# Attention energies from split queries and keys in one float32r pass, with keys and values streamed from DRAM

## The chip, the cores and the metric

The kernel runs on one core of one Trainium2 chip. A core has five engines that run their own instruction streams and meet at semaphores: TensorE (matrix products, PE in the profile; its weight loads are PEld), VectorE (DVE), ScalarE (ACT), GpSimd (POOL) and SyncE (SP), which here only issues DMAs. The metric is the device time of one execution in microseconds, the median of several runs.

## The reference, cut to what matters

Two layers on an image batch x of 4 x 64 x 64 pixels with 256 channels, all in float32. The first is full self-attention inside each image, with queries and keys of 32 channels:

```python
q = x @ Wq + bq            # 4 x 4096 x 32
k = x @ Wk + bk            # 4 x 4096 x 32
v = x @ Wv + bv            # 4 x 4096 x 256
energy = jnp.einsum('bnd,bmd->bnm', q, k)
attn = jax.nn.softmax(energy, axis=-1)
out = gamma * jnp.einsum('bnm,bmc->bnc', attn, v) + inputs
```

The second layer is a depthwise 3x3 convolution to 768 channels, two pointwise products with a GELU between them and a residual, and a local attention over each pixel's 3x3 window. The change touches the first layer only.

## The kernel before, in words

**Tiles and slots.** Each image has 4096 pixels in 8 blocks of 512 (NB). A slot is one block of queries; there are 32, in order, 8 for each image. In a slot the queries of the block meet the keys of all 8 blocks G of their image. The energies stand transposed: 128 keys on the partitions, 512 queries along the free axis. A group is one G: four matmuls (`energy`, L298 to 308) fill four PSUM banks `e` of 128 x 512; `weight` (L310) takes the exponential of two banks at a time on ScalarE into `p`; `product` (L315) multiplies each of the four key tiles' values with `p`, 128 x 512 at a time, into two accumulators `acc`; `add_up` (L329) sums `p` on VectorE into `den` for the softmax's denominator.

**The energies.** The contraction is only 32 long. The four tiles of keys of a block therefore sit in four strips of 32 partitions of one tile `ka` of 128 x 128, the queries are repeated in the four strips of `qa`, and each of the four matmuls uses its own strip of TensorE's rows (32*128 in the profile). They are float32 matmuls. The profile shows every float32 matmul of this kernel as two records.

**Where keys, queries and values come from.** `project_qk(s)` (L231) projects two blocks at once into one PSUM bank, `st` (L242) gets them with the bias added, and small DMAs on SP take the four strips of `ka` from `st` straight into SBUF (L254), 16 KB each, and the queries to a DRAM scratch `packed` (L259). `spread_queries` (L283) brings a block's queries from the scratch four times, into the four strips of `qa`, in the middle of the slot before. `project_v` (L263) makes the values of a block in two halves. Keys and values of a whole image stay in SBUF: 8 buffers of `ka`, 8 of `v`.

**Order of the work.** It is written out by hand. A slot has 16 points, two for each G. At the first of them `energy` is issued for the *next* group, so that the exponentials are a group ahead of the products; then come `weight`, a list of jobs of the second layer for slots further back (`jobs`), `product`, `add_up`, and on VectorE a number of steps of the convolution (`share`). Slots 7, 15 and 23 also project the next image (`nxt`): `project_v` of one block at every second point, `project_qk` of two blocks after the points 1, 5, 9 and 13, with their `xc` loads (L225) ahead. In slot 0 the same is squeezed in for the first image (`early_jobs`, `early`): blocks 0 and 1, then 2 and 3 ahead of the first energies, blocks 4 and 5 after point 1, blocks 6 and 7 after point 3.

**Queues.** Nearly all DMAs are issued on SP, in the order of the program: a DMA that has to wait for its source or for its buffer holds up all those behind it. A buffer of a rotating tile is free again when its last reader is done. On SP stand `renew` (L126, the next slot's block of x, at the start of a slot), the `xc` loads, the key and query copies above, and `out` stores of the second layer after points 4 and 5.

Of the kernel before, what the change touches and what calls it, by code (L numbers as in the profile page):

```python
# [8 lines left out]

F32 = mybir.dt.float32  # L10
AF = mybir.ActivationFunctionType
ALU = mybir.AluOpType
AX = mybir.AxisListType
# [24 lines left out]
GRP = P // CQK  # L38
NG = NT // GRP
SQ = 32  # L40
NJ = NB // SQ
NSLOT = B * NBLK
# [10 lines left out]
def attention_then_perception_kernel(  # L53
# [19 lines left out]
    nc = tc.nc  # L73
# [17 lines left out]
    def unshifted():  # L91
# [105 lines left out]


        queries, keys, values, staged = {}, {}, {}, {}
        packed = tc.dram_tile([CQK, B * N], F32, name="packed")  # L200

        def fetch(s):

# [27 lines left out]
        def project_qk(s):  # L231

            ps = bank("m", f"qk_{s}")
            for kin in range(CH):
                for r in range(2):
                    nc.tensor.matmul(  # L236
                        ps[2 * r * CQK : 2 * (r + 1) * CQK, :],
                        lhsT=wqk[:, kin].rearrange("p s d -> p (s d)"),
                        rhs=staged[s + r][:, kin, :], start=(kin == 0), stop=(kin == CH - 1),
                    )  # L240
            st = tile_of([P, NB], "st", f"st_{s}")
            nc.scalar.activation(st, ps, AF.Identity, bias=bqk2)  # L242
            if s == 0:
                queries[0] = tile_of([P, NB], "qa", "qa_0", 2)
                for j in range(GRP):
                    nc.sync.dma_start(
                        out=queries[0][j * CQK : (j + 1) * CQK, :], in_=st[:CQK, :]
                    )
            for r in range(2):
                at = 2 * r * CQK  # L250
                keys[s + r] = tile_of([P, P], "ka", f"ka_{s + r}", NBLK)
                queue = nc.sync if s + r else nc.scalar
                for j in range(GRP):
                    queue.dma_start(  # L254
                        out=keys[s + r][j * CQK : (j + 1) * CQK, :],
                        in_=st[at + CQK : at + 2 * CQK, bass.ts(j, P)],
                    )
                if s + r:
                    nc.sync.dma_start(  # L259
                        out=packed[:, bass.ts(s + r, NB)], in_=st[at : at + CQK, :]  # L260
                    )

        def project_v(s, pair, tag="m"):  # L263
            xc = staged[s]
            if pair == 0:
                values[s] = tile_of([P, TPB, C], "v", f"v_{s}", NBLK)
            ps = bank(tag, f"v_{s}_{pair}")
            for i in range(2):
                for kin in range(CH):
                    nc.tensor.matmul(  # L270
                        ps[:, i * C : (i + 1) * C],
                        lhsT=xc[:, kin, bass.ts(2 * pair + i, P)], rhs=wv[:, kin, :],
                        start=(kin == 0), stop=(kin == CH - 1),
                    )
            nc.scalar.copy(
                values[s][:, 2 * pair : 2 * pair + 2, :], ps.rearrange("p (t c) -> p t c", c=C)
            )

        def projections(s):
# [3 lines left out]
        def spread_queries(s):  # L283

            queries[s] = tile_of([P, NB], "qa", f"qa_{s}", 2)
            for j in range(GRP):
                nc.sync.dma_start(
                    out=queries[s][j * CQK : (j + 1) * CQK, :],
                    in_=packed[:, bass.ts(s, NB)],
                )  # L290


        energies, weights, sums, accs, lsums, lrdens = {}, {}, {}, {}, {}, {}
# [4 lines left out]
        def energy(s, G):  # L298

            e = epsum.tile([P, GRP, NB], F32, tag="e", name=f"e_{s}_{G}", bufs=1)  # L300
            key = keys[s - s % NBLK + G]
            for j in range(GRP):
                rows = slice(j * CQK, (j + 1) * CQK)
                nc.tensor.matmul(  # L304
                    e[:, j, :], lhsT=key[rows, :], rhs=queries[s][rows, :],
                    start=True, stop=True,
                )
            energies[s, G] = e

# [5 lines left out]
        def product(s, G, half):  # L315
            p = weights[s, G, half]
            first = G == 0 and half == 0
            if first:
                accs[s] = [bank("acc", f"acc_{s}_{c}") for c in range(CH)]
            v = values[s - s % NBLK + G]  # L320
            for i in range(2):
                for c in range(CH):
                    nc.tensor.matmul(  # L323
                        accs[s][c], lhsT=v[:, 2 * half + i, bass.ts(c, P)], rhs=p[:, i, :],
                        start=(first and i == 0),
                        stop=(G == NG - 1 and half == 1 and i == 1),
                    )
# [95 lines left out]
        percs, mixes, hids, hs = {}, {}, {}, {}  # L423
# [14 lines left out]
                thirds[:] = [t[:, i * NB : (i + 1) * NB] for i in range(3)]  # L438
            return thirds.pop(0)

        def spare(name):
            return tile_of([P, TPB, C], "v", name, NBLK).rearrange(
                "p (a t) c -> p a (t c)", a=2
            )

        def perceive(s, steps):

            at = ring(s) - 1
            percs.setdefault(s, {})

            def begin(i):
                if s >= NSLOT - LAG_PERC:

                    if i % 2 == 0:
                        percs[s, i] = spare(f"perc_{s}_{i}")
                    percs[s][i] = percs[s, i - i % 2][:, i % 2, :]
                else:
                    upper, j = divmod(i, MULT)
                    if not upper:
                        mixes[s, j] = perc_tile(f"perc_{s}_{j}")  # L460
                    percs[s][i] = mixes[s, j][:, 2 * upper : 2 * upper + 2, :].rearrange(
                        "p s n -> p (s n)"
                    )
                tap_of(i, 0, 0, RB)

            def tap_of(i, tap, r0, r1):
                half, j = divmod(i, MULT)
                dy, dx = divmod(tap, 3)
                acc = percs[s][i].rearrange("p (h w) -> p h w", w=W)[:, r0:r1, :]
                win = xv[:, half, at + dy + r0 : at + dy + r1, dx : dx + W]  # L470
                wt = wperc[:, half, j, tap : tap + 1]
                if tap == 0:
                    nc.scalar.activation(  # L473
                        acc, win, AF.Identity, bias=bperc[:, half, j : j + 1], scale=wt
                    )
                else:
                    nc.vector.scalar_tensor_tensor(acc, win, wt, acc, ALU.mult, ALU.add)  # L477

            for i, tap, *rows in steps:
# [227 lines left out]
        guides, lvs, near_ws, late, results, totals = [], {}, {}, {}, {}, {}  # L707
# [360 lines left out]
        for i in range(2):  # L1068
            project_v(1, i)
        project_qk(2)  # L1070
        energy(0, 0)
        weight(0, 0, 0)
        weight(0, 0, 1)
# [18 lines left out]
        for slot in range(NSLOT):  # L1092
# [3 lines left out]
            k, a = slot - LAG_HID, slot - LAG_ATT  # L1096
# [50 lines left out]
            for point in range(points):  # L1147
                G, half = divmod(point, 2)
                after = slot + (G + 1) // NG, (G + 1) % NG
                if half == 0:  # L1150
                    if G == NG // 2 and slot + 1 < NSLOT:
                        spread_queries(slot + 1)
                    if after[0] < NSLOT:
                        energy(*after)
# [515 lines left out]
```

## Time and profile before

| | |
|---|---|
| time, median of 3 runs | 3450.98 us (3450.44 to 3451.02) |
| span of the profiled execution | 3448.6 us |
| TensorE busy | 3437.1 us, 100% |
| VectorE busy | 2737.3 us, 79% |
| ScalarE busy | 1063.9 us, 31% |
| DMA, mean | 19 GB/s, 67.05 MB |
| products `acc` (L323) on TensorE | 1835.0 us, 4096 records |
| energies `e` (L304) on TensorE | 292.0 us, 2048 records |
| one plain slot (slots 5, 6, 8 and on) | 102.0 us |
| slots 7, 15, 23, which project the next image | 137.1 us |

The profiled execution's own time is its span; the unprofiled runs lie 2.4 us above it. In the profile a row such as `L304 PE MATMUL e<-qa,ka 32*128 32x512 f32` names the line of the kernel, the engine, the operation, the output and inputs by the program's names and the shape: 32 rows by 128 columns of the array, 512 columns moved. Matmuls are pipelined and their ends are modelled, so the distance between starts says how long TensorE was taken.

### The profile page before, as it was taken

How to read it: one execution, taken by the hardware profiler on the slowest of the kernel's cores; microseconds unless marked ns; L12 is line 12 of the kernel's file. 1: busy time of each engine (PE TensorE's matmuls, PEld its weight loads, DVE VectorE, ACT ScalarE, POOL GpSimd, SP SyncE). 2: the span in 40 equal slices, each digit the busy share in tenths (PEclk: the TensorE clock that was granted, in tenths of full speed). 3: DMA queues.
4: the chain of work that ended last, by engine and by line, in shares of the span. 5: the costliest groups of instructions: out<-in, count | busy, mean ns of one | idle time of the engine just before them, and what ended most of it. 6: DMA issues, size and time to landing. Idle time of an engine off the chain costs nothing.

```text
span 3448.6 us, 33677 instructions
## 1 busy us (share of the span) xinstructions
PE 3437.1 (100%) x12702; PEld 1991.7 (58%) x12702; DVE 2737.3 (79%) x4439; ACT 1063.9 (31%) x1328; POOL 365.7 (11%) x541
## 2 busy tenths in 40 slices
PE   9999999999999999999999999999999999999999
PEld 5445555556555556555555555566656555555555
DVE  2388888767888888876888888887688888888895
ACT  3232333323332233332333322333233333233331
POOL 2000001110111110111001111101110111110021
PEclk9999999999999999999999999999999999999999
DMA  4000000120000000012000000001100000000000
GB/s 107 7 4 10 7 10 16 28 47 18 16 13 10 16 16 16 21 26 46 16 10 16 10 13 16 16 22 29 43 16 16 16 10 7 16 16 18 7 7 26
DMA packets 93274, 67.05 MB, mean 19 GB/s; under 512 B 65872, under 2 KB 71248, under 8 KB 92976
## 3 DMA queue, kind: packets, MB, share of 16 engines
q1 hardware_dynamic: 92432, 64.42, 7.0%
q8 instruction: 102, 1.67, 0.2%
q14 instruction: 68, 0.56, 0.1%
q10 hardware_dynamic: 672, 0.39, 0.0%
HBM read 43.62 MB, written 18.81 MB: 18 GB/s over the span
## 4 chain that ended last, share of the span: by engine, by line
PE 98%; DVE 1%; DMA 0%; SPq 0%; ACT 0%; issue 0%; ACTq 0%; POOL 0%; DVEq 0%
PE acc L323 51%; PE e L304 8%; PE hid_de L582 5%; PE hid_gf L582 5%; PE hid_bc L582 5%; PE lv L895 3%; PE v L270 3%; PE lo L1029 3%; PE s L936 3%; PE hid_a L582 3%; PE dx_ab L534 2%; PE dx_cd L534 1%; PE dx_eg L534 1%; PE qk L236 1%; DVE perc L477 1%; PE dx_f L534 1%
## 5 line engine op out<-in xcount | busy, mean ns | idle before, releaser
L323 PE MATMUL acc<-p,v 128*128 128x512 f32 x4096 | 1835.0, 594 | 0.3 <-DVE o L388 0.3
L323 PEld LDWEIGHTS acc<-p,v 128*128 128x128 f32 x4096 | 768.1, 190 | 809.9 <-issue 793.0
L477 DVE SCALAR_TENSOR_TENSOR perc<-xp,wperc,perc 128x512 f32<-128x512 f32 (+2 forms) x1554 | 1104.5, 773 | 27.5 <-ACT perc L473 27.3
L312 ACT ACTIVATE p<-e 128x1024 f32<-128x1024 f32 x512 | 524.0, 1024 | 1714.9 <-PE e L304 710.7
L337 DVE TENSOR_TENSOR den<-den,p 128x1024 f32<-128x1024 f32 x480 | 587.2, 1223 | 86.2 <-ACT p L312 84.5
L961 POOL TENSOR_TENSOR lp<-lp,near 128x396 f32<-128x396 f32 x60 | 97.0, 1616 | 2487.8 <-ACT lp L956 2487.8
L304 PE MATMUL e<-qa,ka 32*128 32x512 f32 x2048 | 292.0, 640 | 0.0
L304 PEld LDWEIGHTS e<-qa,ka 32*128 32x128 f32 x2048 | 80.0, 182 | 166.2 <-issue 145.3
L582 PE MATMUL hid_de<-perc,wmix 128*128 128x256 f32 x720 | 165.2, 379 | 0.0
L582 PEld LDWEIGHTS hid_de<-perc,wmix 128*128 128x128 f32 x720 | 136.8, 190 | 43.7 <-issue 21.5
L483 DVE TENSOR_TENSOR perc<-perc 128x256 f32<-128x256 f32 x360 | 153.6, 441 | 8.2
L605 ACT ACTIVATE hid<-hid,bup 128x512 f32<-128x512 f32 x120 | 80.1, 714 | 219.5 <-DVE hid L589 219.5
L473 ACT ACTIVATE perc<-xp,bperc,wperc 128x512 f32<-128x512 f32 x192 | 145.3, 805 | 1.8 <-DVE xp L394 1.8
L984 POOL TENSOR_TENSOR lsum<-lsum,lp 128x99 f32<-128x99 f32 (+1 forms) x179 | 130.4, 735 | 11.7
L1029 PEld LDWEIGHTS lo<-lp,lv 128*128 128x128 f32 x732 | 102.9, 191 | 35.1 <-issue 27.2
L895 PE MATMUL lv<-wlv,h 128*128 128x256 f32 x520 | 122.4, 379 | 0.0
L589 DVE TENSOR_TENSOR hid<-hid_bc,hid 128x512 f32<-128x512 f32 x60 | 41.5, 692 | 101.7 <-PE hid_bc L582 101.7
L270 PE MATMUL v<-wv,xc 128*128 128x256 f32 x512 | 116.3, 380 | 0.3 <-DMA wv<-in_w_v 0.3
L270 PEld LDWEIGHTS v<-wv,xc 128*128 128x128 f32 x512 | 96.9, 190 | 28.4 <-issue 15.2
L936 PEld LDWEIGHTS s<-lq,h 128*128 128x128 f32 x520 | 87.1, 188 | 37.3 <-issue 27.4
L895 PEld LDWEIGHTS lv<-wlv,h 128*128 128x128 f32 x520 | 98.7, 190 | 15.5 <-issue 2.2
L1029 PE MATMUL lo<-lp,lv 128*128 128x99 f32 (+1 forms) x732 | 107.4, 295 | 0.0
(195 smaller groups left out, 3098.0 us busy)
## 6 DMA issues: line engine op xcount, KB each, us to landing
xp<-in_x SPq DMA_DIRECT2D x30, 528.0 KB, 4.1
xc<-in_x SPq DMA_DIRECT2D x56, 256.0 KB, 3.7
out<-lo SPq DMA_DIRECT2D x56, 256.0 KB, 2.0
qa<-packed SPq DMA_DIRECT2D x124, 64.0 KB, 2.1
out<-res SPq DMA_DIRECT2D x8, 256.0 KB, 2.0
ka<-st SPq DMA_DIRECT2D x124, 16.0 KB, 1.8
packed<-st SPq DMA_DIRECT2D x31, 64.0 KB, 1.9
wup<-in_w_up SPq DMA_DIRECT2D x1, 1536.0 KB, 6.9
```

What stands on the lines that cost most here:

```text
L270: nc.tensor.matmul(ps[:, i * C : (i + 1) * C], lhsT=xc[:, kin, bass.ts(2 * pair + i, P)], rhs=wv[:, kin, :], start=(kin == 0), stop=(kin = ...
L304: nc.tensor.matmul(e[:, j, :], lhsT=key[rows, :], rhs=queries[s][rows, :], start=True, stop=True,)
L312: nc.scalar.activation(p, energies[s, G][:, 2 * half : 2 * half + 2, :], AF.Exp)
L323: nc.tensor.matmul(accs[s][c], lhsT=v[:, 2 * half + i, bass.ts(c, P)], rhs=p[:, i, :], start=(first and i == 0), stop=(G == NG - 1 and hal ...
L337: nc.vector.tensor_tensor(den, den, p, ALU.add)
L477: nc.vector.scalar_tensor_tensor(acc, win, wt, acc, ALU.mult, ALU.add)
L483: nc.vector.tensor_tensor(t[:, to, :], t[:, a, :], t[:, b, :], op)
L534: nc.tensor.matmul(ps[:, n * C : (n + 1) * C], lhsT=w(j), rhs=values(j), start=(j == 0), stop=(j == kin - 1),)
L582: nc.tensor.matmul(ps[:, n * C : (n + 1) * C], lhsT=w(j), rhs=mixes[s, j][:, kind, :], start=(j == 0), stop=(j == MULT - 1),)
L895: nc.tensor.matmul(ps[:, half * C : (half + 1) * C], lhsT=keys_of(s, t, half, kin), rhs=wlv[:, kin, :], start=(kin == 0), stop=(kin == CH ...
L936: nc.tensor.matmul(ps[:, t * QR * QW : t * QR * QW + rows * QW].rearrange("p (h w) -> p h w", w=QW), lhsT=keys_of(s, t, half, kin), rhs=gu ...
L1029: nc.tensor.matmul(pv[:, rows, columns(half)], lhsT=lvs[block, t, half][:, bass.ts(c, P)], rhs=near_ws[block, half][:, t, of, :], start=(i ...
```

## The change

Each query and key is split into two parts, a high one, written by ScalarE in the float32r format (a float32 with fewer bits of the mantissa), and the low rest, the float32 value minus the high part (a second read of the PSUM bank by ScalarE and a subtraction on VectorE). The 128 partitions of `qa` now hold high, low, high, low of a block's queries, those of `ka` high, high, low, low of its keys; one matmul over all 128 rows then sums the four partial products. An energy group is four matmuls of 128 x 512 marked as float32r, one for each 128 keys.

A key tile is now 128 x 512 for a block, four times as large, and no longer kept: all strips go to DRAM scratches `packed_k` and `packed_q` by four stores for a block each, and `load_keys` brings a block's keys back for each slot and group, two groups ahead, with 3 buffers. Values do likewise: `project_v` stores its halves to `packed_v`, `load_values` fetches a block's 512 KB for each group from slot 1 on, with 3 buffers; the values of the later images pass through small tiles `vs`. `spread_queries` becomes one DMA of 128 partitions. Tiles of the last slots that used free `v` buffers get a name of their own, `late`.

```diff
-        packed = tc.dram_tile([CQK, B * N], F32, name="packed")
+        packed_q, packed_k = (tc.dram_tile([P, B * N], F32, name=n) for n in ("packed_q", "packed_k"))
+        packed_v = tc.dram_tile([P, NSLOT * TPB * C], F32, name="packed_v")
+        Q_PARTS, K_PARTS = (0, 1, 0, 1), (0, 0, 1, 1)
+        def rows_of(j):
+            return slice(j * CQK, (j + 1) * CQK)
...
-            st = tile_of([P, NB], "st", f"st_{s}")
-            nc.scalar.activation(st, ps, AF.Identity, bias=bqk2)
+            high, low = (tile_of([P, NB], tag, f"{tag}_{s}") for tag in ("st", "sl"))
+            nc.scalar.activation(high.bitcast(F32R), ps, AF.Identity, bias=bqk2)
+            nc.scalar.activation(low, ps, AF.Identity, bias=bqk2)
+            nc.vector.tensor_tensor(low, low, high, ALU.subtract)
+            parts = (high, low)
             if s == 0:
                 queries[0] = tile_of([P, NB], "qa", "qa_0", 2)
+                keys[0, 0] = tile_of([P, NB], "ka", "ka_0_0", 3)
+                for j in range(GRP):
+                    nc.scalar.dma_start(
+                        out=keys[0, 0][rows_of(j), :], in_=parts[K_PARTS[j]][CQK : 2 * CQK, :]
+                    )
+                    nc.sync.dma_start(
+                        out=queries[0][rows_of(j), :], in_=parts[Q_PARTS[j]][:CQK, :]
+                    )
+            for r in range(2):
+                at = 2 * r * CQK
                 for j in range(GRP):
                     nc.sync.dma_start(
-                        out=queries[0][j * CQK : (j + 1) * CQK, :], in_=st[:CQK, :]
-                    )
-            for r in range(2):
-                at = 2 * r * CQK
-                keys[s + r] = tile_of([P, P], "ka", f"ka_{s + r}", NBLK)
-                queue = nc.sync if s + r else nc.scalar
-                for j in range(GRP):
-                    queue.dma_start(
-                        out=keys[s + r][j * CQK : (j + 1) * CQK, :],
-                        in_=st[at + CQK : at + 2 * CQK, bass.ts(j, P)],
+                        out=packed_k[rows_of(j), bass.ts(s + r, NB)],
+                        in_=parts[K_PARTS[j]][at + CQK : at + 2 * CQK, :],
                     )
                 if s + r:
-                    nc.sync.dma_start(
-                        out=packed[:, bass.ts(s + r, NB)], in_=st[at : at + CQK, :]
-                    )
+                    for j in range(GRP):
+                        nc.sync.dma_start(
+                            out=packed_q[rows_of(j), bass.ts(s + r, NB)],
+                            in_=parts[Q_PARTS[j]][at : at + CQK, :],
+                        )
+
+        def load_keys(s, G):
+            keys[s, G] = tile_of([P, NB], "ka", f"ka_{s}_{G}", 3)
+            nc.sync.dma_start(out=keys[s, G], in_=packed_k[:, bass.ts(block(s, G), NB)])
+
+        def load_values(s, G):
+            values[s, G] = tile_of([P, TPB, C], "v", f"v_{s}_{G}", 3)
+            nc.sync.dma_start(
+                out=values[s, G].rearrange("p t c -> p (t c)"),
+                in_=packed_v[:, bass.ts(block(s, G), TPB * C)],
+            )
...
-            nc.scalar.copy(
-                values[s][:, 2 * pair : 2 * pair + 2, :], ps.rearrange("p (t c) -> p t c", c=C)
+            nc.scalar.copy(v, ps.rearrange("p (t c) -> p t c", c=C))
+            nc.sync.dma_start(
+                out=packed_v[:, bass.ts(2 * s + pair, 2 * C)], in_=v.rearrange("p t c -> p (t c)")
             )
...
-            key = keys[s - s % NBLK + G]
+            key = keys.pop((s, G))
             for j in range(GRP):
-                rows = slice(j * CQK, (j + 1) * CQK)
                 nc.tensor.matmul(
-                    e[:, j, :], lhsT=key[rows, :], rhs=queries[s][rows, :],
-                    start=True, stop=True,
+                    e[:, j, :], lhsT=key[:, bass.ts(j, P)].bitcast(F32R),
+                    rhs=queries[s].bitcast(F32R), start=True, stop=True,
                 )
...
         project_qk(2)
+        load_keys(0, 1)
         energy(0, 0)
...
                 if half == 0:
+                    ahead = slot + (G + 2) // NG, (G + 2) % NG
+                    if ahead[0] < NSLOT:
+                        load_keys(*ahead)
+                    if 0 < ahead[0] < NSLOT:
+                        load_values(*ahead)
                     if G == NG // 2 and slot + 1 < NSLOT:
                         spread_queries(slot + 1)
                     if after[0] < NSLOT:
```

More of the change, by code (lines that the diff above doesn't have):

```diff
@@ L10 @@
 F32 = mybir.dt.float32
+F32R = mybir.dt.float32r
 AF = mybir.ActivationFunctionType
@@ L250, in project_qk, with block @@
                 at = 2 * r * CQK
-                keys[s + r] = tile_of([P, P], "ka", f"ka_{s + r}", NBLK)
-                queue = nc.sync if s + r else nc.scalar
                 for j in range(GRP):
-                    queue.dma_start(
-                        out=keys[s + r][j * CQK : (j + 1) * CQK, :],
-                        in_=st[at + CQK : at + 2 * CQK, bass.ts(j, P)],
+                    nc.sync.dma_start(
+                        out=packed_k[rows_of(j), bass.ts(s + r, NB)],
+                        in_=parts[K_PARTS[j]][at + CQK : at + 2 * CQK, :],
                     )
                 if s + r:
-                    nc.sync.dma_start(
-                        out=packed[:, bass.ts(s + r, NB)], in_=st[at : at + CQK, :]
-                    )
+                    for j in range(GRP):
[3 more added lines that the diff above has]
+                        )
+        def block(s, G):
+            return s - s % NBLK + G
+        def load_keys(s, G):
[7 more added lines that the diff above has]
+            )
         def project_v(s, pair, tag="m"):
             xc = staged[s]
-            if pair == 0:
-                values[s] = tile_of([P, TPB, C], "v", f"v_{s}", NBLK)
+            if s >= NBLK:
+                v = tile_of([P, 2, C], "vs", f"vs_{s}_{pair}", 2)
+            else:
+                if pair == 0:
+                    values[0, s] = tile_of([P, TPB, C], "v", f"v_0_{s}", 3)
+                v = values[0, s][:, 2 * pair : 2 * pair + 2, :]
             ps = bank(tag, f"v_{s}_{pair}")
@@ L285, in spread_queries @@
             queries[s] = tile_of([P, NB], "qa", f"qa_{s}", 2)
-            for j in range(GRP):
-                nc.sync.dma_start(
-                    out=queries[s][j * CQK : (j + 1) * CQK, :],
-                    in_=packed[:, bass.ts(s, NB)],
-                )
+            nc.sync.dma_start(out=queries[s], in_=packed_q[:, bass.ts(s, NB)])
         energies, weights, sums, accs, lsums, lrdens = {}, {}, {}, {}, {}, {}
@@ L319, in product @@
                 accs[s] = [bank("acc", f"acc_{s}_{c}") for c in range(CH)]
-            v = values[s - s % NBLK + G]
+            v = values[s, G]
             for i in range(2):
@@ L439, in late_tile, with spare @@
             return thirds.pop(0)
[L441 to L444, printed above, removed]
+        def spare(s, name):
+            tag = "v" if s == NSLOT - 1 else "late"
+            return tile_of([P, TPB, C], tag, name, 3).rearrange("p (a t) c -> p a (t c)", a=2)
         def perceive(s, steps):
@@ L454, in begin @@
                     if i % 2 == 0:
-                        percs[s, i] = spare(f"perc_{s}_{i}")
+                        percs[s, i] = spare(s, f"perc_{s}_{i}")
                     percs[s][i] = percs[s, i - i % 2][:, i % 2, :]
```

## The prediction

> **What bounds the kernel now.** I read the page's busy shares, the chain that ended last and the costliest groups first, then TensorE and SP in order of time around the energies.
>
> ```profile
> span 3448.6 us, 33677 instructions
> PE 3437.1 (100%) x12702; PEld 1991.7 (58%) x12702; DVE 2737.3 (79%) x4439; ACT 1063.9 (31%) x1328; POOL 365.7 (11%) x541
> ...
> PE 98%; DVE 1%; DMA 0%; SPq 0%; ACT 0%; issue 0%; ACTq 0%; POOL 0%; DVEq 0%
> ...
> L304 PE MATMUL e<-qa,ka 32*128 32x512 f32 x2048 | 292.0, 640 | 0.0
> ```
>
> TensorE is the bound all the way: 98% of the chain, hardly a gap. What shortens its stream shortens the kernel; what makes it wait is added. The energies are 2048 records, 256 groups of 8. One group in order of time (columns: start us, length us, engine, line, what):
>
> ```profile
> 1237.23 1.88 PE L323 MATMUL acc<-p,v 128*128 128x512 f32 x4
> 1239.04 1.14 PE L304 MATMUL e<-qa,ka 32*128 32x512 f32 x8
> 1240.11 1.99 PE L534 MATMUL dx_ab<-hid,wup 128*128 128x256 f32 x8
> 1241.94 3.60 PE L323 MATMUL acc<-p,v 128*128 128x512 f32 x8
> ```
>
> Starts tell more than modelled ends. Eight acc records fill 1241.94 to 1245.38, where the next group begins: 0.43 each. The four at 1237.23 last 1.81 until the energies start, 0.09 more than 4 x 0.43. The energies hold 1239.04 to 1240.11, 1.07. Eight 256-column records should take 8 x 0.2155 = 1.72 but take 1.83: 0.11 more. So a group costs 0.09 + 1.07 + 0.11 = 1.27, twice a fifth of a microsecond of it at the borders; 256 groups are 325 us, more than the 292 of their row.
>
> SP in slot 15, after the fourth pair of blocks of the next image was projected at 1622.77:
>
> ```profile
> 1623.63 2.41 SPq L254 DMA_DIRECT2D ka<-st  x4
> 1626.09 0.58 SPq L259 DMA_DIRECT2D packed<-st  x1
> 1626.77 2.41 SPq L254 DMA_DIRECT2D ka<-st  x4
> 1629.22 0.58 SPq L259 DMA_DIRECT2D packed<-st  x1
> 1629.91 0.61 SPq L126 DMA_DIRECT2D xp<-in_x  x1
> ```
>
> Ten small stores hold SP for 6.28 us, 0.63 each. Now nothing urgent stands behind them.
>
> **What the Trainium skill says.** "FP8 and Floating Point Precision", TensorE Precision Notes: true FP32 takes four passes, the reduced form of FP32 one. The trace fits the four: a program matmul of 512 columns is two records of 0.43, four times 0.214. No trace here shows a float32r matmul. "TensorEngine Tiling (Array Packing)", Key Properties: changing the tiling mode drains TensorE; the 0.09 and 0.11 at the two borders agree. "TensorE: Matmul & The Clock Gate", Part 1: after some 3.4 us idle the clock halves until some 3.4 us of work have passed; here the 20 opening matmuls of 128 columns take 4.33 us, 0.216 each, what 256 columns take later. "DMA: Bandwidth & Descriptors", Anatomy of one DMA: about 2 us fixed plus the bytes; 64 KB land here in 2.1 us (qa), 256 KB in 2.0 to 3.7 (out, xc).
>
> **The energies (removed: 256 groups of four row-tiled FP32 matmuls; added: 256 groups of four full-height float32r).** One pass of 512 columns should be 0.2155, as a 256-column FP32 record is now (also two passes' worth of 256 columns, with its 0.19 weight load hidden). Four are 0.862, with no change of tiling at either border. Bounds: 0.862 with clean borders; 0.862 + 0.20 if the change of number format costs what the change of tiling did; 4 x 0.43 = 1.714 if float32r streams no faster than a record does today. I take 0.862: the weight loads are as hidden as those of 256-column records. Gain 256 x (1.269 - 0.862) = 104.2 us.
>
> **The streams.** Each group now loads 256 KB of keys and, after slot 0, 512 KB of values on SP: 768 KB per 12.3 us, 62 GB/s, 504 issues of about 0.4 us. A value load waits on SP for the products of the group before, whose buffer it takes, and its own products come two groups later, over 15 us even in the short slots 1 and 2. A key load stands right behind the previous value load and has two groups too. Out stores wait on SP for VectorE only 1.7 us after their point's products begin; the xp load for the next slot is ready at points 8 to 10 and now comes after point 13. So in the 28 plain slots nothing is late. Values stored from vs add 64 issues; ScalarE's copy waits for the store two before it, which SP has done by then. Price if this cover were gone: each microsecond of lateness per group is 256 us.
>
> **The second read of q and k.** 16 more activations (0.69, row L242) and 16 subtractions (0.69, as L339): 11 us each, on ScalarE at 31% and on VectorE, which sits idle just then (for 4.9 us around the second pair of slot 15, 7.6 around the third). Cost zero but for the stores behind them: the first store of a low part can go 2.35 us after the projection's end.
>
> **Stores ahead of urgent key loads, three image changes.** A pair of blocks now needs 16 stores where it had 10, and a key load stands behind them. From the projection's end: st stored from +0.86, low parts from +2.35, stores done at 2.35 + 14 x 0.63 = +11.2. Then, except after the fourth pair, two xc loads (+12.2), then the key load. Alone, I take 2.6 us to landing; behind two xc, whose 512 KB keep the DMA engines busy 2.6 us (1513.27 to 1515.89), 4.2. The energies that need it, with 0.41 off for the faster group: first pair +20.2, lands +16.4, no wait; second +16.4, none; third +13.8 (1593.75 to 1607.98), waits 2.6; fourth +11.45 (energies at 1622.77, then at 1634.63), lands +13.8, waits 2.3. Some 5 us for each of slots 7, 15 and 23: 15 us. Bounds: 6 if landing is 1.6 quicker, 27 if 2 slower.
>
> **The opening.** Keys of block 1 came by four direct copies; now they go to the scratch and back, behind everything SP has queued:
>
> ```profile
> 15.39 1.94 PE L236 MATMUL qk<-xc,wqk 128*64 128x512 f32 x8 [0.44 <-ACT v L275]
> 17.26 1.14 PE L304 MATMUL e<-qa,ka 32*128 32x512 f32 x8
> 18.33 3.72 PE L270 MATMUL v<-wv,xc 128*128 128x256 f32 x16
> 21.98 1.14 PE L304 MATMUL e<-qa,ka 32*128 32x512 f32 x8
> ...
> 35.35 1.14 PE L304 MATMUL e<-qa,ka 32*128 32x512 f32 x8
> ...
> 48.10 1.14 PE L304 MATMUL e<-qa,ka 32*128 32x512 f32 x8
> ...
> 59.69 1.14 PE L304 MATMUL e<-qa,ka 32*128 32x512 f32 x8
> ```
>
> SP has the four qa copies out at 13.7 (the low part holds them until 11.8). Twelve stores: 21.3; three value stores of 0.5: 22.8; sixteen stores: 32.9. The load of keys 1 lands at 35.7 instead of letting energies 1 run at 21.98: 13.7 late, with TensorE idle so long that the clock halves, 1.7 more. Energies 2: 35.7 + 0.86 + 6.9 (products) + 3.44 + 1.75 (qk, v) + 1.7 = 50.4. The 16 stores of the pair 4, 5 run to 59.8, two value stores and a key load to 61.2, and only then go the xc loads of blocks 6 and 7; from their first issue to energies 3 took 7.7 (40.41 to 48.10), so 68.9. Sixteen stores again, keys 4 land at 82.9, so energies 4 come there instead of at 59.69: 23.2 late, with 1.6 gained by four groups in between. Waits in sum 24.8 us. Bounds: 15 if the issues run at the 0.4 of a lone one, 33 if the clock and the landings are worse.
>
> **Sum.** 3448.6 - 104.2 + 15 + 24.8 = 3384.2 for the profiled execution; the median of the runs is 2.4 above its span, so 3386.6, say 3387. At the end, the tiles named late take the place of freed v buffers: no work moved. In the last slot VectorE is busy 129.44 of 148.00 us, so up to 2 us of its gain may not show.
>
> **Rivals.** (1) The other side: float32r at 0.43 per 512 columns, because a record streams four-byte numbers no faster than today's. Groups cost 1.714, +114 us, and stalls of some 35: 3600. The even point is 1.269 - 40/256 = 1.113 per group, 0.278 per matmul. For it: no run shows the pass rate. Against it: 256-column records move four-byte numbers at 0.2155 for two passes. (2) The borders stay, 0.2 per group: gain 53.5, 3437. The trace ties them to the change of tiling, which goes. (3) The waits are hidden after all, SP issuing quicker: 3347 to 3365. (4) VectorE becomes the bound: 86.85 busy of 102.00 us per plain slot, which shrinks to 98.7; it holds. (5) The streams run late in plain slots, about 3450 to 3550; the slack of two groups speaks against it.
>
> **How the numbers follow.** Likeliest case 66%, own range 3365 to 3410; (2) 11%, (3) 8%, (1) 12%, (5) with (4) 3%. The range 3348 to 3440 leaves out (1), (5) and tails of the others. Faster 0.83, slower 0.14, within 0.2% (about 7 us, what a measurement of this kernel can tell from none) 0.03, from a bad mix of (2) and the waits.
>
> **What would show it.** Energy records: half as many (1024), 0.216 apart, the neighbours' extra 0.09 and 0.11 gone. Plain slots 98.8 instead of 102.0. Energies 1 to 4 near 36, 50, 69 and 83 us, waiting for DMA ka. In slots 7, 15, 23 waits of 2 to 3 us on ka after the third and fourth pair. Wrong if the energy matmuls lie over 0.25 apart, or if TensorE waits for ka or v in plain slots.

## The result, and the profile after

The changed kernel takes 3399.51 us, the median of its runs (3398.79 to 3400.99), against 3450.94 for the kernel before beside it: a ratio of 0.9852, 95% interval 0.9838 to 0.9866. That is 51 us less. The forecast was 3387; the time lies inside its range, 12.5 us above the point. Between the spans the distance is 13.7: 3397.9 against a forecast of 3384.2 (the forecast added 2.4 from span to median, here it is 1.6). Those 13.7 are what is left of a gain that fell short by about 29, of two losses that were foretold 8 and 12 too large, and of one of 4 that was put at nothing. The rest of this document is about them.

The page of the changed kernel: span, busy shares, shares of the chain that ended last, the row of the energies.

```profile
span 3397.9 us, 32797 instructions
PE 3367.3 (99%) x11678; PEld 2117.9 (62%) x11678; DVE 2746.6 (81%) x4455; ACT 1071.8 (32%) x1344; POOL 347.5 (10%) x541
...
PE 92%; DVE 6%; SPq 1%; DMA 1%; issue 0%; ACT 0%; ACTq 0%; POOL 0%; DVEq 0%; POOLq 0%
...
L334 PE MATMUL e<-qa,ka 128*128 128x512 f32 x1024 | 365.0, 478 | 11.0 <-DMA ka<-packed_k 11.0
```

TensorE is still the bound, but no longer alone: 6% of the chain now runs over VectorE (1% before). That share says where the chain passes and not what it costs; the slots concerned lose some 4 us in all, as shown below. The energies are 1024 records in place of 2048: a float32r matmul is one record where a float32 matmul is two. Their row's busy time has grown from 292.0 to 365.0 us all the same. Ends are modelled, and here the first record of a group is also shown as starting inside the last product; busy time is no measure of what a group costs. From the first `acc` of a point to the first `acc` of the next it can be read cleanly. TensorE in order of time, the point that the prediction showed (start us, length us, engine, line, what):

```profile
1226.19 3.62 PE L353 MATMUL acc<-p,v 128*128 128x512 f32 x8
1229.25 1.48 PE L334 MATMUL e<-qa,ka 128*128 128x512 f32 x4
1230.57 1.89 PE L563 MATMUL dx_ab<-hid,wup 128*128 128x256 f32 x8
1232.30 1.02 PE L353 MATMUL acc<-p,v 128*128 128x512 f32 x2
```

The point takes 1232.30 - 1226.19 = 6.11 us. In the kernel before the same two marks are 6.45 apart, 1235.49 to the 1241.94 that the prediction showed:

```profile
1235.49 3.62 PE L323 MATMUL acc<-p,v 128*128 128x512 f32 x8
```

One group of energies is 0.34 cheaper here, and not the 0.41 of the prediction. A plain slot has gone from 102.0 to 99.5.

TensorE's waits (engine, line, what it waited for: us in total, times, longest):

```profile
PE e L334 <- DMA ka<-packed_k: 11.0, 4, 8.4
PE qk L245 <- DMA xc<-in_x: 5.1, 2, 4.7
...
PE dps L406 <- DVE parts L388: 1.2, 6, 0.2
...
PE c L908 <- DVE edge L897: 0.7, 3, 0.2
```

8.4 of the 11.0 and the second line are the opening. The last two lines are new: near the end of some slots TensorE waits for VectorE.

The opening on TensorE, energies 1 to 4:

```profile
31.93 2.05 PE L334 MATMUL e<-qa,ka 128*128 128x512 f32 x4 [8.44 <-DMA ka<-packed_k]
...
45.24 1.28 PE L334 MATMUL e<-qa,ka 128*128 128x512 f32 x4
...
65.74 1.52 PE L334 MATMUL e<-qa,ka 128*128 128x512 f32 x4
...
77.25 1.25 PE L334 MATMUL e<-qa,ka 128*128 128x512 f32 x4
```

They come at 31.9, 45.2, 65.7 and 77.3 (before: 22.0, 35.4, 48.1, 59.7; foretold: about 36, 50, 69, 83). The granted clock stood at half from 25.5 to 35.8 and from 59.7 to 66.5. SP behind the first and second pair of blocks shows why the energies are earlier than foretold:

```profile
13.50 1.05 SPq L268 DMA_DIRECT2D packed_k<-st  x2
14.59 0.90 SPq L268 DMA_DIRECT2D packed_k<-sl  x2
...
23.01 0.42 SPq L274 DMA_DIRECT2D packed_q<-st  x1
23.47 0.43 SPq L274 DMA_DIRECT2D packed_q<-sl  x1
...
28.64 0.43 SPq L284 DMA_DIRECT2D ka<-packed_k  x1
```

Behind one another the stores go at 0.47 us, not at 0.63, and the load of keys 1 goes out at 28.64 rather than 32.9.

### The profile page after: what moved, and what is told of

It reads as the page before. It is cut to its first block, busy times and chain, and to the rows that moved or that the text cites. A ratio compares the mean times of both kernels' runs of the same rounds, so it can differ in the third digit from the quotient of the medians.

```text
span 3397.9 us, 32797 instructions
## 1 busy us (share of the span) xinstructions
PE 3367.3 (99%) x11678; PEld 2117.9 (62%) x11678; DVE 2746.6 (81%) x4455; ACT 1071.8 (32%) x1344; POOL 347.5 (10%) x541
## 4 chain that ended last, share of the span: by engine, by line
PE 92%; DVE 6%; SPq 1%; DMA 1%; issue 0%; ACT 0%; ACTq 0%; POOL 0%; DVEq 0%; POOLq 0%
PE acc L353 48%; PE e L334 7%; PE hid_de L611 5%; PE hid_gf L611 5%; PE hid_bc L611 5%; PE lv L924 3%; DVE perc L506 3%; PE lo L1058 3%; PE v L304 3%; PE hid_a L611 2%; PE s L965 2%; PE dx_cd L563 1%; PE dx_ab L563 1%; PE dx_eg L563 1%; DVE den L367 1%; PE g_cd L563 1%
## 5 line engine op out<-in xcount | busy, mean ns | idle before, releaser
L342 ACT ACTIVATE p<-e 128x1024 f32<-128x1024 f32 x512 | 523.9, 1024 | 1673.6 <-PE e L334 745.9
L334 PE MATMUL e<-qa,ka 128*128 128x512 f32 x1024 | 365.0, 478 | 11.0 <-DMA ka<-packed_k 11.0
L990 POOL TENSOR_TENSOR lp<-lp,near 128x396 f32<-128x396 f32 x60 | 89.7, 1494 | 2426.1 <-ACT lp L985 2426.1
L334 PEld LDWEIGHTS e<-qa,ka 128*128 128x128 f32 x1024 | 190.4, 190 | 141.2 <-issue 107.7
L1013 POOL TENSOR_TENSOR lsum<-lsum,lp 128x99 f32<-128x99 f32 (+1 forms) x179 | 123.1, 694 | 11.7
L924 PEld LDWEIGHTS lv<-wlv,h 128*128 128x128 f32 x520 | 98.7, 190 | 15.5 <-issue 2.2
```

The costliest lines, as they stand in the source:

```text
L334: nc.tensor.matmul(e[:, j, :], lhsT=key[:, bass.ts(j, P)].bitcast(F32R), rhs=queries[s].bitcast(F32R), start=True, stop=True,)
L342: nc.scalar.activation(p, energies[s, G][:, 2 * half : 2 * half + 2, :], AF.Exp)
L924: nc.tensor.matmul(ps[:, half * C : (half + 1) * C], lhsT=keys_of(s, t, half, kin), rhs=wlv[:, kin, :], start=(kin == 0), stop=(kin == CH ...
```

## The experiments

**The streams without the one pass.** Are the keys and values from DRAM free in the plain slots? The changed kernel, with the energies again as float32 on 32 rows:

```diff
-    e[:, j, :], lhsT=key[:, bass.ts(j, P)].bitcast(F32R),
-    rhs=queries[s].bitcast(F32R), start=True, stop=True,
+    e[:, j, :], lhsT=key[rows_of(j), bass.ts(j, P)],
+    rhs=queries[s][rows_of(j), :], start=True, stop=True,
```

> The changed kernel with its stores and streams as they are, but each energy matmul again a float32 one on 32 rows, strip j of the keys against strip j of the queries. It leaves out three of the four partial products of each energy, so its output is another one; the instructions' sizes are those of the kernel before. Theory A (the waits and the energy pass are two separate terms): groups cost 1.27 us again, and the time is that of the kernel before plus the waits of the streams, some 18 us in the opening and 2 to 4 at the three image changes: 3469 to 3475. Theory B (with longer groups TensorE hides the waits, because the loads get more time): 3451 to 3458.

Measured: 3470.09 us (3468.68 to 3472.56), ratio 1.0056 (1.0039 to 1.0073). Its point takes the old 6.45 again (1253.66 to 1260.11 in order of time on TensorE):

```profile
1253.66 3.62 PE L353 MATMUL acc<-p,v 128*128 128x512 f32 x8
...
1260.11 2.31 PE L353 MATMUL acc<-p,v 128*128 128x512 f32 x5
```

Plain slots take 102.0 us as before. Slot 1 begins 18.2 us later than in the kernel before (131.5 against 113.4), slots 15 and 23 take 0.8 and 1.6 longer. These three, 20.5, are the whole loss of 20.2 between the two spans (3468.8 and 3448.6; slot 26 of the kernel before had itself taken 0.3 more than its like). In plain slots the streams cost nothing, and the waits don't hide behind longer groups: theory A.

**The one pass without the streams.** The kernel before, with float32r matmuls over all 128 rows of its `ka` tile; each then sums over all four strips, which the scale of the exponential evens out in size:

```diff
...
-    e[:, j, :], lhsT=key[rows, :], rhs=queries[s][rows, :],
+    e[:, j, :], lhsT=key.bitcast(F32R), rhs=queries[s].bitcast(F32R),
...
-    nc.scalar.activation(p, energies[s, G][:, 2 * half : 2 * half + 2, :], AF.Exp)
+    nc.scalar.activation(p, energies[s, G][:, 2 * half : 2 * half + 2, :], AF.Exp, scale=0.5)
```

> The kernel before, without scratches and streams, its four energy matmuls of a group in float32r over all 128 rows of its 128 x 128 key tile. Each sums the four strips, so its energies are other numbers, and the exponential takes them times 0.5 to stay in range. Theory A (0.2315 us from matmul to matmul is float32r's own pace): the same 0.2315 without any stream, 0.31 us less per group on average, 256 groups, 79 us: 3372. Theory B (the streams slow the matmuls, which would run at 0.2155 without them): 0.2155 from start to start and 16 us more gain, 3356.

Measured: 3379.16 us (3378.69 to 3379.4), ratio 0.9791 (0.9775 to 0.9808), 71.8 less than before. The row of the energies, one group in order of time, and a wait:

```profile
L304 PE MATMUL e<-qa,ka 128*128 128x512 f32 x1024 | 364.0, 477 | 0.0
```

```profile
1211.31 1.48 PE L304 MATMUL e<-qa,ka 128*128 128x512 f32 x4
1212.63 1.89 PE L534 MATMUL dx_ab<-hid,wup 128*128 128x256 f32 x8
```

```profile
PE dps L376 <- DVE parts L358: 1.2, 6, 0.2
```

Without any stream a group starts 1.32 us ahead of `dx_ab`, as with the streams (1229.25 to 1230.57), and the starts of its second, third and fourth matmul stand as far apart: 0.2315. So the pitch does not come from contention with the streams. The gain fell 7 short of theory A's 79, for reasons that the section on the prediction gives. The two halves of the change add up: -71.8 + 19.2 = -52.6, measured together -51.4. The waits for VectorE are here too, so they belong to the faster energies and not to the streams.

**Half as many columns.** Does the weight load, 190 ns busy in its row, hold the pitch at 0.2315?

```diff
-    e[:, j, :], lhsT=key[:, bass.ts(j, P)].bitcast(F32R),
-    rhs=queries[s].bitcast(F32R), start=True, stop=True,
+    e[:, j, cols], lhsT=key[:, bass.ts(j, P)].bitcast(F32R),
+    rhs=queries[s][:, cols].bitcast(F32R), start=True, stop=True,
```

with `cols` the two halves of the 512, one after the other.

> The changed kernel with each energy matmul cut into two of 256 columns, with the same result. If the pace of 0.2315 is set by the weight load (0.19 busy) and something around it, 256 columns take 0.2315 too and a group 1.85 us, 0.93 more: some 3400 + 237 = 3637. If it is set by the columns, 256 of them take 0.116 to 0.125 unless the load then binds: 0.15 to 0.20 each, 1.2 to 1.6 a group, 3470 to 3570.

Measured: 3407.05 us in one run; both expectations missed. TensorE at the same point, and the page's row of the weight loads:

```profile
1230.08 3.62 PE L355 MATMUL acc<-p,v 128*128 128x512 f32 x8
...
1236.22 3.60 PE L355 MATMUL acc<-p,v 128*128 128x512 f32 x8
```

```profile
L336 PEld LDWEIGHTS e<-qa,ka 128*128 128x128 f32 x2048 | 276.6, 190 | 116.4 <-issue 105.9
```

The point takes 6.14 in place of 6.11, with twice the weight loads. 256 columns stand 0.119 apart: less than the 0.190 that a load is shown busy. So the load does not set the 0.2315. Two points, 0.2315 and 0.119, give 0.44 ns for a column and 6.5 ns for a matmul besides. If a record of the float32 products is two passes, as the prediction reads it, a column takes 0.4285/1024 = 0.418 ns for a pass, and a float32r column is about 5% slower. Why is not settled, but the opening of the changed kernel narrows it down. There the clock stood at half, and each of these lines begins with the first record that its view takes in:

```profile
32.50 1.48 PE L334 MATMUL e<-qa,ka 128*128 128x512 f32 x3
...
33.78 2.44 PE L353 MATMUL acc<-p,v 128*128 128x512 f32 x3
...
34.63 1.06 PE L353 MATMUL acc<-p,v 128*128 128x512 f32 x1
```

Three float32r matmuls take 1.28, 0.427 each, and a record of the products 0.85, twice as much. At half clock a float32r matmul thus costs what one of two passes costs, and the difference is gone. So it is not in the number of passes, and what makes it at full clock does not slow down with the clock.

**The opening repaired.** The prediction put the cost of the opening on the queue of SP: keys that go through DRAM behind the stores, and `xc` loads behind the same stores. Keys 1 and 2 are copied straight from the projection, the `xc` of blocks 4 to 7 go ahead of the stores, keys 3 and 4 are loaded early. The high and low parts of the first four blocks get `late` tiles, in which they can wait for their stores:

```diff
...
+            if s in (0, 2):
+                G, at = (1, 3 * CQK) if s == 0 else (2, CQK)
+                keys[0, G] = tile_of([P, NB], "ka", f"ka_0_{G}", 3)
+                for j in range(GRP):
+                    nc.sync.dma_start(
+                        out=keys[0, G][rows_of(j), :], in_=parts[K_PARTS[j]][at : at + CQK, :]
+                    )
+                stores.append((s, parts))
+                return
+            store(s, parts)
...
-            fetch(s)
-            fetch(s + 1)
+            if s == 4:
+                for i in range(4):
+                    fetch(s + i)
+                while stores:
+                    store(*stores.pop(0))
+                load_keys(0, 3)
+            else:
+                load_keys(0, 4)
             project_qk(s)
```

> The changed kernel with another order in the opening, the same result: keys of blocks 1 and 2 are copied straight from the projection, the xc loads of blocks 4 to 7 go out next, the stores of blocks 0 to 3 after them, and keys 3 and 4 are loaded ahead of the later stores. Theory A (SP's queue of stores costs the opening 18 us on the path that sets the end): energies 1 near 22, 2 near 35, 3 near 47, 4 near 58 us, slot 1 begins near 112 instead of 129, time 3381 to 3385. Theory B (that time would be taken back later, as VectorE or the DMAs catch up only behind it): less than 6 us gained, over 3393.

Measured: 3382.57 us (3380.85 to 3383.02), ratio 0.9801 (0.9784 to 0.9817), 16.9 below the changed kernel. The opening on TensorE:

```profile
21.73 1.28 PE L357 MATMUL e<-qa,ka 128*128 128x512 f32 x4
...
49.13 2.05 PE L357 MATMUL e<-qa,ka 128*128 128x512 f32 x4 [3.63 <-DMA ka<-packed_k]
...
61.74 1.27 PE L357 MATMUL e<-qa,ka 128*128 128x512 f32 x4
```

Energies 1 and 2 (at 33.8) come as early as in the kernel before, 3 and 4 one and two microseconds later, and slot 1 begins at 113.9 in place of 129.4. Keys and `xc` loads that stood in SP's queue behind the stores were the loss. The run changes both at once, so it doesn't say how much belongs to either.

**The later stores behind the loads.** In slots 7, 15 and 23 the sixteen stores of a pair stand ahead of a key load. SP in slot 15 of the changed kernel, third pair (with the wait of TensorE that follows in the second fence):

```profile
1581.84 2.31 SPq L268 DMA_DIRECT2D packed_k<-st  x2
...
1588.15 0.91 SPq L284 DMA_DIRECT2D ka<-packed_k  x1
```

```profile
1592.15 1.20 PE L334 MATMUL e<-qa,ka 128*128 128x512 f32 x4 [1.02 <-DMA ka<-packed_k]
```

The edit gives these stores a place behind the next loads (`stores` collects them in `project_qk`):

```diff
                         load_values(*ahead)
+                    while slot >= NBLK - 1 and stores:
+                        store(*stores.pop(0))
```

> The changed kernel with one thing moved: the sixteen stores of each pair of blocks of the second to fourth image go to SP only after the next point's loads of keys and values, instead of ahead of them. Nothing is left out. Theory A (the small wait left in slots 7, 15 and 23, about 3.7 us in all against three plain slots, is the key load that stands behind the stores): the wait on ka of about 1 us in slot 15 goes, slots 7, 15 and 23 lose about 1 us each, time 3399.5 - 3.5 = about 3396. Theory B (what is left there is the projections' own work on TensorE and its halts at changed tile widths, and the stores' place in the queue is free): slots 7, 15 and 23 stay at 136 to 137 us, time within 1 us of 3399.5.

Measured: 3397.51 us (3394.98 to 3398.15), ratio 0.9844 (0.9831 to 0.9858), 2.0 less. SP around the same place, and TensorE's wait for keys:

```profile
1578.71 0.91 SPq L292 DMA_DIRECT2D ka<-packed_k  x1
```

```profile
PE e L342 <- DMA ka<-packed_k: 8.4, 1, 8.4
```

The load goes out 10 us earlier, counted from the slot's start, and only the wait of the opening is left. Slots 7, 15 and 23 take 135.4 each, where they took 135.9, 136.7 and 136.9: 3.3 us by the slots. The medians show 2.0 of it, since their openings differ by about 1 us (slot 1 began 1.1 later in this profile).

**VectorE's margin.** Slots 10, 11, 18, 19, 26 and 27 take 100.2 to 100.4 in the changed kernel (102.1 before, where a plain slot took 102.0). They hold four more edge instructions on VectorE. The end of slot 10 on TensorE:

```profile
1082.64 0.38 PE L406 MATMUL dps<-parts,fold 128*128 128x32 f32 x2 [0.20 <-DVE parts L388]
```

`dps` stands ahead of the next group of energies and waits for sums that VectorE makes after all its other work. The wait shown, 0.20, is less than the loss: this last point of slot 10 takes 10.64, and 10.18 in a plain slot; the point with `c` takes 4.86 and 4.59. So some of the convolution's steps go to earlier points:

```diff
-            share = [6, 7, 7, 5, 4, 3, 3, 3, 2, 2, 4, 5, 5, 4, 0, 0]
+            share = [6, 7, 7, 5, 4, 3, 3, 3, 3, 4, 4, 5, 4, 2, 0, 0]
```

> The changed kernel with another split of the convolution's 60 steps over a slot's points: up to three of them move from points 12 and 13 to points 8, 9 and 10 (3, 4, 4, 5, 4, 2 at points 8 to 13 where there were 2, 2, 4, 5, 5, 4). Nothing is left out. Theory A (VectorE's margin ran out in the six slots 10, 11, 18, 19, 26, 27, which have four more edge instructions, so that TensorE waits for VectorE's sums at the slot's end): moved earlier, the same instructions fill VectorE's idle time before, these six slots go from 100.2 to 99.5 us, and the time from 3399.5 to about 3395.5. Theory B (these slots are longer for another reason, such as the edges' own place): they stay at 100.2, and the time within 1 us of 3399.5; if the moved steps push other work late, it is a few us longer.

Measured: 3404.17 us (3402.52 to 3405.41), ratio 0.9866 (0.9851 to 0.9881), 4.7 slower than the changed kernel; the end of theory B came. The costliest of TensorE's waits for VectorE:

```profile
PE g_cd L563 <- DVE lq L577: 5.8, 28, 0.6
```

The waits of `dps` and `c` are gone and the six slots took 99.9, but now 28 slots wait for `lq`: each plain slot grew from 99.5 to 99.8. The one step put at point 8 stands ahead of `lq` on VectorE, where before only 0.28 us were free:

```profile
1249.71 0.74 DVE L506 SCALAR_TENSOR_TENSOR perc<-xp,wperc,perc 128x512 f32<-128x512 f32 x1
1250.37 0.48 DVE L577 SCALAR_TENSOR_TENSOR lq<-g_ab,small,lq 128x256 f32<-128x256 f32 x1
```

The next run leaves point 8 alone and puts both steps at point 9, where VectorE of the changed kernel sat idle for 1.90 us (ahead of the `lq` that waits for `g_eg`):

```diff
-            share = [6, 7, 7, 5, 4, 3, 3, 3, 2, 2, 4, 5, 5, 4, 0, 0]
+            share = [6, 7, 7, 5, 4, 3, 3, 3, 2, 4, 4, 5, 5, 2, 0, 0]
```

> The changed kernel with the convolution's steps split 2, 4, 4, 5, 5, 2 at points 8 to 13: two steps move from point 13 to point 9, and none to point 8. Nothing is left out. The run with 3, 4, 4, 5, 4, 2 took the six long slots from 100.2 to 99.9 but every other slot from 99.5 to 99.8, with TensorE waiting for VectorE's lq in 28 slots. Theory A (the step at point 8 stood ahead of lq, where VectorE has only 0.28 us free, and the end of slots 10, 11, 18, 19, 26, 27 lacks margin as supposed): with 1.4 us of steps put where VectorE idles 1.9 us at point 9, plain slots are back at 99.5, the six go to 99.5 too, 3399.5 - 4 = about 3395.5, and the waits of dps and of c for VectorE are gone. Theory B (any of these steps moved earlier comes back as another wait of TensorE for VectorE, which has nothing left to give in such a slot): plain slots stay above 99.5, time 3399 to 3404.

Measured: 3394.25 us (3392.55 to 3394.48), ratio 0.9837 (0.9823 to 0.985), 5.3 less than the changed kernel. The same point in slot 10:

```profile
1080.44 0.30 PE L406 MATMUL dps<-parts,fold 128*128 128x32 f32 x2
```

`dps` no longer waits, plain slots take 99.5 and the six 99.6. Against the changed kernel the six give 4.1 us by their lengths. The medians differ by one more; in the two profiles the opening and the image changes are shorter too, by 0.9 and 1.7, with nothing moved there, so that is put down to scatter.

**All three repairs.** Opening, later stores behind the loads, and the steps moved; in the opening the keys of block 3 are also stored and loaded ahead of all other stores. First with the split that held `lq` up:

> The changed kernel with the opening of the run before (keys 1 and 2 copied straight from the projection, x of blocks 4 to 7 fetched ahead of the stores), with the four stores of block 3's keys alone ahead of its load, with the later images' stores behind the next loads, and with the convolution's steps split anew. Nothing is left out. Theory A (the three waits are independent, and what each edit saves adds up): 3399.5 - 17 - 2 to 3 (block 3's keys no longer late by 3.6) - 3.5 - 4 = about 3372, below both kernels and below the single pass in the kernel before (3379). Theory B (the later ones were only the slack of the same queue, or one saving takes the other's place): about 3380, as with the opening alone.

Measured: 3385.52 us (3384.75 to 3386.62), ratio 0.9812 (0.9798 to 0.9825). Both expectations were missed. Plain slots took 99.8 again: 5.8 us of waits for `lq` in 28 slots are more than the six slots give. Then with the other split:

> The run with all three edits (opening, later stores behind the next loads, split of the steps), with the split of 2, 4, 4, 5, 5, 2 in place of the one that held lq up. Nothing is left out. Theory A (the edits are independent once lq is not held up): the opening alone was 3382.6; less 4 for the six slots and 2 for the stores behind the loads, about 3376.5, below the single pass put into the kernel before (3379.2). Theory B (VectorE's work moved comes back as waits): 3382 to 3386.

Measured: 3376.26 us (3374.66 to 3376.59), ratio 0.9784 (0.977 to 0.9797). That is 23.3 below the changed kernel; the three repairs alone gave 16.9, 2.0 and 5.3, 24.2 together. This kernel computes all that the reference asks and is faster than both. The longest of its waits:

```profile
PE v L332 <- ACT sl L256: 3.0, 1, 3.0
```

No wait for keys is left, but storing block 3's keys first mostly moved a stall: energies 3 come at 45.4 in place of 49.1, then `v` waits 3.0 for a low part (energies 4: 60.4, with the opening's repair alone 61.7, so 1.3 is gained). What ScalarE waited for there was not tried.

## Why the prediction was right and wrong

Against the predicted sum, term by term, from the two profiled executions:

| step of the prediction | foretold, us | found, us |
|---|---|---|
| energies, 256 groups | -104.2 | about -75 |
| opening | +24.8 | about +17 |
| three image changes | +15 | +3.3 |
| VectorE at slot ends | 0 | +4.1 |
| sum on 3448.6 | 3384.2 | about 3398 (span 3397.9) |

**The energies** came as foretold in kind (one record a matmul at the pace of about one pass, clean borders) and were off in two sizes. The 1.27 of a group before is right, but its borders are 0.09 + 0.11, one fifth of a microsecond and not "twice a fifth". What the rest was, the starts of the group that the prediction showed tell, taken in by two narrow views:

```profile
1239.04 0.71 PE L304 MATMUL e<-qa,ka 32*128 32x512 f32 x4
...
1239.58 0.61 PE L304 MATMUL e<-qa,ka 32*128 32x512 f32 x4
```

The eight records went in two rounds of four, the four strips of a round side by side (0.007 apart), the rounds 0.53 apart. Two rounds at the products' 0.4285 would take 0.86; four float32r matmuls take 4 x 0.2315 = 0.926. So fewer passes saved nothing here: side by side on a quarter of the rows each, the float32 matmuls had made up for theirs. The gain is what a group spent beyond 0.86, about 0.20 at its borders and 0.21 within. This is read from starts; no run kept the strips without that extra time.

"One pass of 512 columns should be 0.2155" measured 0.2315: four times 0.016, 0.064 of a group, and it made 0.34 of the foretold 0.41. The change of number format at the borders, for which a bound held 0.20 ready, cost nothing that shows: of the point's 6.11, eight products take 3.43 and `dx_ab` 1.73, which leaves 0.95, hardly more than the four matmuls. "No change of tiling at either border" held for six of the eight groups of a plain slot. The point of the group ahead of `c`, whose tile is one column wide, went only from 4.73 to 4.58, and the last point, with `dps` ahead of the group, from 10.45 to 10.18. Six times 0.34 to 0.35, 0.15 and 0.27 make the 2.48 of a slot. In slots 7, 15 and 23 the `qk` matmuls, 64 columns wide (128*64), stand right ahead of four groups and the slots gain 1.66: a group behind `qk` gains 0.15 (point 1 of slot 15: 13.91 to 13.76), and one between `qk` and `c` loses 0.05. The Trainium skill, "TensorEngine Tiling (Array Packing)", Key Properties, ties the drain to a change of tiling mode; that agrees with a border that goes where both neighbours are 128*128 and stays beside 128*64 and 128*1. It doesn't explain the 0.27 of the group behind `dps`, which is 128*128 too; that stays open. In all: 32 x 2.48 = 79.4, less 3 x 0.8 for those slots, less 1.4 and 0.6 by which slots 0 and 31 fall short, about 75.

**The opening** was right in mechanism; the term mis-sized is the issue pitch. 0.63 was read from a mix, eight of whose ten DMAs were copies inside SBUF, and the new stores, all to DRAM, went at 0.47. The kind of transfer is not all of it: the two stores to DRAM in that mix took 0.58 as well, each behind a copy, and the first pair of stores in the changed kernel, behind a `qa` copy, took 1.05 where the next took 0.90 (13.50 and 14.59 above). What stands ahead counts too, and the kernel before never had two of these stores in a row. Twenty-eight stores stood ahead of the load of keys 1, 28 x 0.16 = 4.5 us, and it went out 4.3 earlier than foretold. Slot 1 begins at 129.4, and with the one pass alone at 112.2: 17.2 us. The run with the direct copies shows SP's queue as the cause. The clock was priced at 1.7 us once. It fell to half twice, 2.1 and 4.6 us after TensorE's last matmul, and came back 3.9 and 6.7 us after TensorE went on; the prediction took some 3.4 for each.

**The image changes** fell with the same 0.16 us: sixteen stores end 2.6 us sooner, the foretold waits were 2.3 and 2.6, so they should nearly vanish (a landing 1.6 quicker, the prediction's lower bound, leaves about 5 us by its own figures, not 6). What was left, 3.3 us, came irregularly: 0.1 and 0.4 in slot 7, 1.3 after the third pair of slot 15, 1.55 after the fourth of slot 23. In slot 15 one pair of stores held SP 2.31 us. That the waits belong to these stores is shown by the run that moves them.

**VectorE**: "it holds" was wrong in six slots, by about 0.7 us each. The prediction compared busy sums, 86.85 of 98.7 us. What counted was the margin of one chain at the slot's end: the convolution's last steps, the edges, the sums, `dps`. The run with two steps at point 9 takes the wait away.

**The rivals.** Float32r at 0.43 (1) is excluded by 0.2315. Borders that all stay (2) are excluded by the clean six of eight, though a part was true. Waits hidden after all (3) is the direction in which opening and image changes erred. VectorE as the bound (4) came in small. Streams late in plain slots (5) is excluded by the unchanged 102.0 of the streams alone. The errors had opposite signs, 29 too good and 4 left out against 8 and 12 too bad; the nearness of the forecast is partly luck.

## What to carry to other kernels

Price an issue from a row of the same kind of transfer behind the same kind, and a matmul from a row of the same number format; where the trace has none, widen the bounds. A neighbour's row was 34% and 7% off here, and 256 repetitions turn 7% into 16 us. Before counting passes, look at the starts for what already runs side by side: here the gain lay in borders and gaps, not in passes. When the bounding engine gets faster, look past the busy shares for the other engine's last chain ahead of it: its slack at that one place is the margin, and work moved to make room there needs a gap that is long enough, or it comes back as a wait in every slot. Here data sent through DRAM cost nothing in the steady state with two groups of slack, and in the opening, where there is none, it waited for all that its queue held.

## What the runs showed that was not expected

- A float32r matmul of 512 columns takes 0.2315 us and one of 256 columns 0.119: about 0.44 ns a column, against 0.418 for a pass of the float32 products. At half clock both take 0.427 for 512 columns and a pass.
- Four float32 matmuls on strips of 32 rows ran side by side, so that they streamed in about the time of four float32r matmuls on all rows.
- Weight loads shown busy for 190 ns kept up with matmuls 0.119 us apart.
- DMAs from 32 partitions of SBUF to DRAM were issued 0.47 us apart behind one another; the mix of the kernel before, mostly copies inside SBUF, went 0.63 apart, and a store to DRAM behind such a copy held SP for 0.58. The four `qa` copies of the changed kernel, also inside SBUF, still go 0.6 apart.
